# Layer 0's first step: queries, keys and values by whole products, and the x sums of the first sequence formed in step 4

## The chip, the cores and the metric

The kernel runs on one core of a Trainium2 chip. A core has five engines that work side by side, each through its own list of instructions in order: TensorE (PE, matrix products and transposes), VectorE (DVE), ScalarE (ACT), GpSimd (POOL) and SyncE (SP, which here only issues DMA transfers). They wait for one another by semaphores. The metric is the device time of one execution in microseconds (us); less is better. A kernel is timed as the median of several runs.

## The reference

Two transformer layers on x of 4 sequences x 512 rows x 512 columns, all in float32. Each layer normalizes x and adds an attention and a mixture of experts. What matters here is the attention of layer 0:

```
xn = layernorm(x)
q  = rope(rmsnorm(xn @ Wq + bq))        # 16 heads of 128
lk = rope(rmsnorm(xn @ Wlk + blk))      # keys and values of the local window
lv = xn @ Wlv + blv
w  = softmax(xn @ Wcmp + bcmp) over every 4 rows     # compressed entries
entries = sum over 4 rows of w * xn
ck = rope(rmsnorm(entries @ Wk + bk));  cv = entries @ Wv + bv
ctx = top8_attention(q, ck, cv) + window_attention(q, lk, lv)
out = ctx/2 @ Wo + bo
```

The mixture of experts of layer 0 picks two of eight experts for each row by `xn @ Wr`.

## The kernel before

**Tiling.** x lies on chip as 16 tiles of 128 rows (`acc`); sequence b has tiles 4b to 4b + 3. `layernorm(n)` (line 195) makes one tile: row statistics (`bn_stats`, L201, then L203 and L204 on VectorE), the power -1/2 on GpSimd (L205), the scaled rows (L211), a write of these to memory for the experts (L212), four transposes on TensorE (L217) and a copy on ScalarE into `xnT` (L218). `start_sequence(n)` calls it.

**Steps.** Layer 0's attention runs 32 steps: 8 groups of 2 heads, and in each group the 4 sequences; step i is group i // 4 and sequence i % 4. A step projects 512 rows of `xnT` with the group's weights: `w_a` holds the columns of the two heads' queries and of the first head's keys (384 in all), `w_b` the two heads' values and the second head's keys. `project(i)` returns the parts of this. Then come `scores`, `turn`, `context`, `turn_context` and `output` of the step.

**Seven products for eight.** The rows are split in two halves, the columns of x in two halves, and the columns of the weights into `w_a` and `w_b`. The plain product of these 2 x 2 blocks has eight block products. `project` uses a scheme with seven (p1 to p7, `product`, line 552, matmuls at L555), which costs sums: four sums of x (`sums_x`, L545 to L548), sums of the weights per group (`combine_weights`, L106), and sums of products while these leave PSUM (L590, L591, L597, L598, L604, L611 to L619). A block product is 2 blocks of 128 rows x 2 of contraction; one such product shows as two matmul instructions in the profile, so a step has 14 x 4 = 56. `finish` then takes the squares (L459, ScalarE), the norms (L460, L461, GpSimd), the rotation (L468 to L471, VectorE) and the scale (L569, ScalarE); `turn_queries` and `turn_keys` transpose (L575, L581).

**x sums.** They are the same for all groups. In steps 0 to 3 VectorE forms them and SP writes them to memory (`xsd`, L550); from step 4 on `load_sums` reads them back (L530) into four tiles with one buffer each. `combine_weights` overwrites the first half of `w_b` and the bias of `w_b` in place.

**Compressed keys.** `compress(b)` is a generator in four stages, each taken by a `next`: the softmax weights of every four rows (from the logits of `first_logits`, L227 to L234; L479 to L490), their spread to all partitions by a product and the weighted sums of x (`entT`, L493 to L498), keys and values (L503 to L510), the turned keys `ckT` (L513, L514).

**Order.** Ahead of the loop over steps stands a prologue, written out by hand, with the projections of step 0, the four stages of `comp[0]`, the layernorms of tiles 4 to 7 and the logits of sequences 0 and 1. In the loop's iteration i the parts of `project(i + 1)` stand between the parts of the attention of step i, and a list of jobs (`run0`) adds layernorms, routing and experts at places (i, t). In iteration 3 begin the choice of experts (`choose`, `place`). A planner then orders each engine's instructions: of those that its model of time takes as ready, the one earliest in the program goes first, so an instruction that is ready early can float ahead. `keep_in_program_order` pins one behind the instruction written before it on its engine. PSUM tiles with the tag "mm" (all the products here) have three buffers.

Of the kernel before, what the change touches and what calls it, by code (L numbers as in the profile page):

```python
# [12 lines left out]
F32 = mybir.dt.float32  # L13
I32 = mybir.dt.int32
AF = mybir.ActivationFunctionType
ALU = mybir.AluOpType
# [4 lines left out]
P = 128  # L21
B, S, HID = 4, 512, 512
T = B * S
NT = T // P
TC = S // P
KC = HID // P
NH, D = 16, 128
# [17 lines left out]
def two_layers(ctx: ExitStack, tc: tile.TileContext, a: dict, out: bass.AP, large: bass.AP):  # L45
# [3 lines left out]
    V, G, A, PE = nc.vector, nc.gpsimd, nc.scalar, nc.tensor  # L49
# [11 lines left out]
    wk0 = layer0.enter_context(tc.tile_pool(name="att0", bufs=2))  # L61
    setup = ExitStack()

    sp0 = setup.enter_context(tc.tile_pool(name="setup", bufs=2, side="right"))


    def psum(tag, name):
        return ps.tile([P, 512], F32, tag=tag, name=name, bufs={"mm": 3, "sc": 3, "tr": 2}[tag])
# [120 lines left out]
    def unrotated():  # L189


        tc.keep_in_program_order(V.memset(turned, 1.0))
        V.tensor_scalar(turned[R:P, :], wcol[R:P, 0:1], wcol[R:P, 1:2], D * math.sqrt(D), ALU.mult, ALU.mult)

    def layernorm(n, pool, bank):

        pin = tc.keep_in_program_order if n < TC else (lambda x: x)
        st = small.tile([P, 6], F32, tag="st", name=f"st_{n}")  # L200
        pin(V.bn_stats(st, acc[:, n, :]))  # L201
        mv = small.tile([P, 2], F32, tag="mv", name=f"mv_{n}")
        V.bn_aggr(mv, st)  # L203
        V.tensor_scalar(mv[:, 1:2], mv[:, 1:2], 1e-5, None, ALU.add)  # L204
        G.tensor_tensor(mv[:, 1:2], mv[:, 1:2], nhalf[:, 0:1], ALU.pow)  # L205
        made = {}

        def rows():
            tag = "ctx" if n in (2, 3) else "xn"
            xn = made["xn"] = (wk0 if n in (2, 3) else pool).tile([P, HID], F32, tag=tag, name=f"xn_{n}")  # L210
            pin(V.tensor_scalar(xn, acc[:, n, :], mv[:, 0:1], mv[:, 1:2], ALU.subtract, ALU.mult))  # L211
            (nc.scalar if TC <= n < 2 * TC else nc.sync).dma_start(out=xnd[ts(n, P), :], in_=xn)  # L212

        def turn():
            xn, tr = made["xn"], bank("tr", f"trx_{n}")
            for k in range(KC):
                pin(PE.transpose(tr[:, ts(k, P)], xn[:, ts(k, P)], ident))  # L217
            A.copy(xnT[:, :, ts(n, P)], tr.rearrange("p (k t) -> p k t", k=KC))  # L218
        return rows, turn
# [304 lines left out]

    def load_sums(i):

        for n in range(4):
            xs[n] = wk0.tile([P, 2, 256], F32, tag=f"x{n}", name=f"x{n}_{i}", bufs=1)
            if i >= B:
                nc.sync.dma_start(out=xs[n].rearrange("p k t -> p (k t)"), in_=xsd[steps[i][1], n])  # L530

    def project(i):
# [3 lines left out]
        g, b = steps[i]  # L536
# [4 lines left out]
        u, qb, sq = {}, {}, {}  # L541

        def sums_x():
            if i < B:
                V.tensor_tensor(xs[2], x11, x21, ALU.subtract)  # L545
                V.tensor_tensor(xs[0], x21, x22, ALU.add)
                V.tensor_tensor(xs[1], xs[0], x11, ALU.subtract)
                V.tensor_tensor(xs[3], x12, xs[1], ALU.subtract)  # L548
                for n in range(4):
                    nc.sync.dma_start(out=xsd[b, n], in_=xs[n].rearrange("p k t -> p (k t)"))  # L550
# [64 lines left out]
        def fifth():  # L615
            u2 = u["u2"]
            for c in range(2):
                p3 = product("p3", xs3, w_b[:, 2:4, :], c).rearrange("p (h d) -> p h d", d=D)
                V.tensor_tensor(lv[:, c, :, 0:D], p3, by_head(u2)[:, c], ALU.add)  # L619
            x = lv[:, :, 2, 0:D]  # L620
            ss = squares(x, TC, wk0, f"{i}_k", float(D))
            rotate(x, t1[:, :, 2, :], t2[:, :, 2, :], TC, wk0, f"{i}_k")
            for h in range(HG):
                norm_k[(i, h)] = [ss[:, t : t + 1] if h else sq[t // 2][:, ds(t % 2 * 3 + 2, 1)] for t in range(TC)]

        xs0, xs1, xs2, xs3 = (xs[n] for n in range(4))
        return qkT, sums_x, first, second, third, fourth, fifth, turn_queries, turn_keys

# [121 lines left out]
    def first_logits(b):  # L750
        def get(rows_):
            V.tensor_copy(lg0[:, ts(b, TC), :], rows_[:, :, 1:])
        lr, turn = logits(b, wr, sp0, "r0", get, psum)
        turn()
        row_w[b] = lr[0:1, :]
# [4 lines left out]
        return logits(b, rout["rw"], pool, "r1", get, bank)[1]  # L760

    def start_sequence(n):
        for f in layernorm(n, sp0, psum):
            f()

    def add_bo(n):
# [92 lines left out]
        jobs0.append(((len(steps) - 1, b), lambda b=b: second_logits(b, rout["pool"], psum)()))  # L859
    run0 = schedule(jobs0)  # L860

    load_sums(0)
    qkT, sums_x, first, second, third, fourth, fifth, turn_queries, turn_keys = project(0)
    start_sequence(0)
    start_sequence(1)
    def rest():
# [21 lines left out]
        part = load(const, "part", [P, 1], a["c_part"])  # L888
        tables()

    first(rest)
    combine_weights(0)
    unrotated()
    sums_x()
    first_logits(0)
    second(0)
    turn_queries(0)
    second(1)
    third()
    next(comp[0])  # L900
    start_sequence(4)
    start_sequence(5)
    fourth()
    next(comp[0])
    turn_queries(1)
    start_sequence(6)
    fifth()
    next(comp[0])
    turn_keys(0)
    start_sequence(7)  # L910
    next(comp[0])
    first_logits(1)
    for i, (g, b) in enumerate(steps):
        if b == 0:
# [1146 lines left out]
```

## Time and profile before

| | us |
|---|---|
| three runs, median | 2111.65 (2110.91 to 2112.95) |
| profiled execution | 2114.76 |
| its span, first to last instruction | 2112.8 |
| TensorE busy | 2057.1 (97%) |
| VectorE busy | 1463.7 (69%) |
| ScalarE busy | 872.0 (41%) |
| GpSimd busy | 732.8 (35%) |
| mean granted TensorE clock | 0.996 |
| first product of step 0 | starts at 9.77 |
| first scores of step 0 | start at 58.97 |
| first scores of step 3 | start at 200.93 |

The profile is of one execution. All positions in time count from the first instruction. PE is TensorE, PEld its loads of weights, L is a line of the kernel. A line of the timeline gives the start, the duration of the merged stretch, the engine, the line, the operation, output and inputs, the shape, how many instructions, and in brackets how long the engine was idle before it and what ended that. A line of the waits gives who waited for whom, the total, how often, and the longest. A line of the windows gives a stretch, its length, the busy time of PE, PEld, DVE, ACT and POOL with the number of instructions, the granted clock of TensorE, the busy share of the DMA engines, and GB/s. The name `wB` stands there both for the weights of that name and for the spread weights of `compress`.

### The profile page before, as it was taken

What the parts mean: (1) busy time and instruction counts of PE and PEld (TensorE: products, weight loads), DVE (VectorE), ACT (ScalarE), POOL (GpSimd) and SP (SyncE); (2) the same over time, 40 slices, a digit from 0 to 9 for tenths busy, and PEclk for the clock granted to TensorE, in tenths of its full rate; (3) what the DMA queues carried; (4) which work ended last, traced back from release to release, by engine and by line L of the source; (5) the groups of instructions that cost most, each with busy time, mean ns of one, the idle gap of its engine ahead of it and who ended that gap; (6) DMA issues with size and microseconds to landing.
All of it is one profiled execution on the core that took longest, in us unless ns stands there. A gap on an engine that the chain in (4) does not pass through costs nothing.

```text
span 2112.8 us, 27908 instructions
## 1 busy us (share of the span) xinstructions
PE 2057.1 (97%) x9138; PEld 1229.1 (58%) x9138; DVE 1463.7 (69%) x3514; ACT 872.0 (41%) x2661; POOL 732.8 (35%) x722
## 2 busy tenths in 40 slices
PE   7999999999999999999999999999999999999988
PEld 4566666666666666666666666665334445445443
DVE  7978967666766766666676778787486555556775
ACT  3444544444444444444443444444243332333332
POOL 3322244443323333333332344453113432332650
PEclk9999999999999999999999999999999999999999
DMA  7201123323332333343233222221316775673551
GB/s 251 76 31 58 39 97 114 143 100 110 126 127 95 121 136 100 110 141 111 95 134 129 76 70 71 70 90 61 115 57 220 258 239 181 217 239 122 143 167 56
DMA packets 95818, 258.73 MB, mean 122 GB/s; under 512 B 12913, under 2 KB 25201, under 8 KB 85681
## 3 DMA queue, kind: packets, MB, share of 16 engines
q0 software_dynamic: 25712, 139.48, 20.0%
q1 hardware_dynamic: 68800, 115.29, 16.4%
q10 hardware_dynamic: 1152, 2.10, 0.3%
q8 instruction: 75, 1.23, 0.2%
q14 instruction: 79, 0.64, 0.1%
HBM read 212.52 MB, written 44.30 MB: 122 GB/s over the span
## 4 chain that ended last, share of the span: by engine, by line
PE 78%; DVE 9%; issue 4%; ACT 4%; POOL 3%; DMA 2%; SPq 0%; ACTq 0%; POOLq 0%; DVEq 0%
PE p L555 22%; PE hp_r L419 13%; PE op L722 10%; PE st L647 4%; PE qp L1090 3%; PE st L1114 3%; PE sp L638 2%; PE cx L1128 2%; PE trm_r L409 2%; PE o L1197 2%; ACT sq L459 2%; PE ca L691 2%; PE vp L1050 1%; PE trq L575 1%; PE trs L673 1%
## 5 line engine op out<-in xcount | busy, mean ns | idle before, releaser
L722 PE MATMUL op<-Wo,cT 128*128 128x512 f32 x512 | 230.4, 598 | 4.9 <-DVE lv L619 3.1
L419 PE MATMUL hp_r<-we_r,xT_r 128*128 128x512 f32 x520 | 235.0, 595 | 0.0
L655 POOL TENSOR_TENSOR lT<-lT,lmask 128x512 f32<-128x512 f32 (+1 forms) x128 | 156.4, 1234 | 182.5 <-ACT lT L651 182.3
L384 POOL DMA_INDIRECT xr_r<-xnd,rows_r x78 | 101.1, 1296 | 293.0 <-PE trm_r L409 243.9
L555 PE MATMUL p<-wB,x 128*128 128x384 f32 x512 | 176.4, 488 | 4.1 <-DVE u L611 3.4
L555 PE MATMUL p<-wT,x 128*128 128x384 f32 x512 | 179.5, 493 | 0.7 <-DVE wT L106 0.7
L555 PE MATMUL p<-wA,xnT 128*128 128x384 f32 x512 | 173.3, 489 | 0.4 <-DVE u L590 0.4
L722 PEld LDWEIGHTS op<-Wo,cT 128*128 128x128 f32 x512 | 92.0, 190 | 114.6 <-issue 77.2
L459 ACT ACTIVATE sq<-qb 128x128 f32<-128x128 f32 x384 | 119.0, 310 | 89.9 <-DVE qb L604 35.3
L419 PEld LDWEIGHTS hp_r<-we_r,xT_r 128*128 128x128 f32 x520 | 94.8, 190 | 104.5 <-issue 96.0
L1116 ACT ACTIVATE pT<-st 128x1024 f32<-128x1024 f32 x128 | 123.9, 1018 | 68.4 <-PE st L1114 57.4
L725 DVE TENSOR_TENSOR acc<-acc,op 128x512 f32<-128x512 f32 x128 | 87.7, 685 | 72.3 <-PE op L722 72.0
L555 PEld LDWEIGHTS p<-wB,x 128*128 128x128 f32 x512 | 94.0, 190 | 67.5 <-issue 9.6
L555 PEld LDWEIGHTS p<-wT,x 128*128 128x128 f32 x512 | 95.2, 193 | 63.3 <-issue 8.9
L555 PEld LDWEIGHTS p<-wA,xnT 128*128 128x128 f32 x512 | 95.0, 192 | 59.8 <-DVE u L590 1.6
L411 ACT COPY xT_r<-trm_r 128x512 f32<-128x512 f32 x78 | 45.3, 581 | 203.4 <-PE trm_r L409 168.0
L569 ACT ACTIVATE qb<-qb,ss 128x128 f32<-128x128 f32 x256 | 81.9, 390 | 111.6 <-POOL ss L461 108.5
L651 ACT ACTIVATE lT<-st,ss 128x256 f32<-128x256 f32 (+1 forms) x128 | 46.8, 448 | 177.8 <-PE st L647 177.7
L647 PE MATMUL st<-qkT 128*128 128x256 f32 (+1 forms) x512 | 109.3, 354 | 0.0
L434 POOL DMA_INDIRECT row_r<-yd,slot_r x64 | 74.8, 1169 | 96.2 <-DVE row_r L1226 35.5
L647 PEld LDWEIGHTS st<-qkT 128*128 128x128 f32 x512 | 92.0, 191 | 10.9 <-issue 1.0
L461 POOL TENSOR_TENSOR ss<-ss,nhalf 128x6 f32<-128x6 f32 x64 | 95.2, 1488 | 5.3
(320 smaller groups left out, 4334.3 us busy)
## 6 DMA issues: line engine op xcount, KB each, us to landing
x<-xsd SPq DMA_DIRECT2D x112, 256.0 KB
yd<-yr_r SPq DMA_DIRECT2D x78, 256.0 KB
wA<-in_wA SPq DMA_DIRECT2D x16, 384.0 KB
wB<-in_wB SPq DMA_DIRECT2D x16, 384.0 KB
xnd<-xn SPq DMA_DIRECT2D x24, 256.0 KB
accd<-acc SPq DMA_DIRECT2D x18, 256.0 KB
acc<-in_x SPq DMA_DIRECT2D x16, 256.0 KB
Wo<-in_Wo SPq DMA_DIRECT2D x8, 512.0 KB
```

The source lines that it names most:

```text
L384: G.indirect_dma_start(out=out, out_offset=None, in_=src, in_offset=at_rows(idx[:, i : i + 1]))
L419: PE.matmul(hp, lhsT=xT[:, k, :], rhs=w[:, ts(k, HID)], start=(k == 0), stop=(k == KC - 1))
L434: G.indirect_dma_start(out=x, out_offset=None, in_=self.yd, in_offset=at_rows(self.r.slot[:, k, n : n + 1]))
L459: A.activation(sq, x[:, h, :], AF.Square, accum_out=ss[:, h : h + 1])
L461: G.tensor_tensor(ss, ss, nhalf[:, 0:n], ALU.pow)
L555: PE.matmul(p, lhsT=x[:, k, ts(c, P)], rhs=w[:, k, :], start=(k == 0), stop=(k == 1))
L569: A.activation(x[:, j, :], x[:, j, :], AF.Copy, scale=sq[t][:, j : j + 1])
L647: PE.matmul(st[:, ds((t % 2) * 256, n)], lhsT=qkT[:, HG + h, ts(t, P)], rhs=qkT[:, h, ds(t * P, n)], start=True, stop=True)
L655: G.tensor_tensor(dst, dst, lmask.rearrange("p a w j -> p (a w j)")[:, 0:n], ALU.mult)
L722: PE.matmul(op, lhsT=cT[:, h, ts(t, P)], rhs=wo[:, h, :], start=(h == 0), stop=(h == HG - 1))
L725: V.tensor_tensor(acc[:, n, :], acc[:, n, :], op, ALU.add)
L1116: A.activation(pt[:, ts(pair, 2), :], st, AF.Exp, scale=SCALE1)
```

## The change

Step 0 no longer uses the seven products. A new function `whole` makes, for a half of the rows (two blocks of 128), the full product with `w_a` or with `w_b` over all four blocks of the contraction and adds the bias as it leaves PSUM: 16 block products of 128 rows, 64 matmul instructions. `project(0)` returns this in place of the seven products' parts, and the end of `fifth` becomes `local_norms`, which step 0 calls by itself. Step 0 forms no x sums and has no `load_sums`. Steps 1 to 3 are as before; step 4, the next step of sequence 0, forms the sums of sequence 0 and writes them, where it read them before. Step 8 and later read them as before. In the prologue, `combine_weights(0)` stands behind the last whole product, the logits of sequence 0 behind the second pair of query blocks, the first stage of `comp[0]` between the two pairs of value blocks, and the layernorms of tiles 4 to 7 behind the turned keys. For tiles 8 to 15 `start_sequence` pins the row statistics to their place (`hold`).

```diff
-    def layernorm(n, pool, bank):
+    def layernorm(n, pool, bank, hold=False):
...
-        pin(V.bn_stats(st, acc[:, n, :]))
+        (tc.keep_in_program_order if hold else pin)(V.bn_stats(st, acc[:, n, :]))
...
     def load_sums(i):
...
-            if i >= B:
+            if i > B:
                 nc.sync.dma_start(out=xs[n].rearrange("p k t -> p (k t)"), in_=xsd[steps[i][1], n])
...
         def sums_x():
-            if i < B:
+            if i <= B:
                 V.tensor_tensor(xs[2], x11, x21, ALU.subtract)
...
+            local_norms()
+
+        def local_norms():
             x = lv[:, :, 2, 0:D]
...
+        def whole(part_, cs, between=lambda: None):
+
+            made = []
+            for c in cs:
+                p = psum("mm", f"pw{part_}_{c}")[:, 0 : 3 * D]
+                for k in range(KC):
+                    PE.matmul(p, lhsT=xnT[:, k, ds(b * S + c * P, P)], rhs=(w_a, w_b)[part_][:, k, :],
+                              start=(k == 0), stop=(k == KC - 1))
+                made.append((c, p))
+            between()
+            for c, p in made:
+                if part_:
+                    V.tensor_tensor(lv[:, c, :, 0:D], p.rearrange("p (h d) -> p h d", d=D),
+                                    b2[:, 1, :].rearrange("p (h d) -> p h d", d=D), ALU.add)
+                    continue
+                if c % 2 == 0:
+                    qb[c // 2] = wk0.tile(rows3, F32, tag="qb", name=f"qb{c // 2}_{i}")
+                V.tensor_tensor(qb[c // 2][:, c % 2, :], p, b2[:, 0, :], ALU.add)
+                if c % 2:
+                    finish(c // 2)
+
+        if i == 0:
+            return qkT, whole, local_norms, turn_queries, turn_keys
...
     def start_sequence(n):
-        for f in layernorm(n, sp0, psum):
+
+        for f in layernorm(n, sp0, psum, hold=n >= 2 * TC):
             f()
...
-    load_sums(0)
-    qkT, sums_x, first, second, third, fourth, fifth, turn_queries, turn_keys = project(0)
+    qkT, whole, local_norms, turn_queries, turn_keys = project(0)
...
-    first(rest)
+    whole(0, (0, 1), rest)
+    unrotated()
+    whole(0, (2, 3))
+    first_logits(0)
+    whole(1, (0, 1))
+    next(comp[0])
+    turn_queries(0)
+    whole(1, (2, 3))
     combine_weights(0)
-    unrotated()
-    sums_x()
-    first_logits(0)
-    second(0)
-    turn_queries(0)
-    second(1)
-    third()
-    next(comp[0])
-    start_sequence(4)
-    start_sequence(5)
-    fourth()
+    local_norms()
     next(comp[0])
     turn_queries(1)
+    turn_keys(0)
+    start_sequence(4)
+    next(comp[0])
+    start_sequence(5)
+    next(comp[0])
     start_sequence(6)
-    fifth()
-    next(comp[0])
-    turn_keys(0)
     start_sequence(7)
-    next(comp[0])
     first_logits(1)
```

## The prediction

> **What bounds the kernel now.** I read the page's engine table first. TensorE (PE) is busy for 97% of the span and VectorE (DVE) for 69%, so over the whole program TensorE sets the time, and a change can win only where TensorE waits, runs at a lower clock, or does less.
>
> ```profile
> PE 2057.1 (97%) x9138; PEld 1229.1 (58%) x9138; DVE 1463.7 (69%) x3514; ACT 872.0 (41%) x2661; POOL 732.8 (35%) x722
> ...
> PE   7999999999999999999999999999999999999988
> ```
>
> The span is 2112.8, so TensorE idles 55.7 us in all; much of that lies in the first of the 40 slices, in which the first step's projections are made. So the second view is the waits of TensorE over the first 200 us:
>
> ```profile
> PE trx L217 <- DVE xn L211: 8.0, 3, 5.9
> PE trq L575 <- ACT qb L569: 3.1, 3, 2.0
> PE wB L493 <- DVE wd L490: 1.5, 1, 1.5
> ```
>
> The 5.9 and 1.9 in the first line are the load and the layernorm of the first rows, ahead of any product, and are not touched. The third view is TensorE's timeline (start, duration, what, idle before it and its releaser), from the second product group on:
>
> ```profile
> 18.04 3.60 PE L227 MATMUL lg_r<-xnT,wr 128*9 128x512 f32 x8 [0.76 <-ACT xnT L218]
> 22.34 0.41 PE L234 MATMUL trg_r<-ident,lr_r 9*128 9x9 f32 x4 [0.69 <-ACT lr_r L229]
> 24.79 0.33 PE L575 MATMUL trq<-ident,qb 128*128 128x128 f32 x1 [2.04 <-ACT qb L569]
> ...
> 26.86 8.39 PE L555 MATMUL p<-wT,x 128*128 128x384 f32 x16 [0.70 <-DVE wT L106]
> 35.09 2.74 PE L555 MATMUL p<-wT,xnT 128*128 128x384 f32 x8
> ...
> 43.64 0.33 PE L575 MATMUL trq<-ident,qb 128*128 128x128 f32 x1 [0.85 <-ACT qb L569]
> 44.23 0.63 PE L575 MATMUL trq<-ident,qb 128*128 128x128 f32 x3 [0.25 <-ACT qb L569]
> ```
>
> Read the 16 matmuls at 26.86 against the 8 at 35.09: the first take 0.51 us each, the others 0.32. TensorE had only the small transposes to do from 21.6 on, then waited for the weight sums, and started those products at half clock. The fourth view, windows of 2 us (last but two: granted clock), says so, and shows VectorE full at its start (third pair):
>
> ```profile
> 24.00:26.00 2.00, 1.21 (x8) 1.00 (x8) 1.72 (x5) 1.28 (x4) 0.30 (x1) 1.00 1.06 406
> 26.00:28.00 2.00, 1.30 (x4) 0.84 (x3) 2.00 (x4) 0.97 (x3) 0.00 (x0) 0.51 1.05 389
> 28.00:30.00 2.00, 2.00 (x4) 1.01 (x3) 0.98 (x4) 0.00 (x0) 0.00 (x0) 0.50 1.05 386
> 30.00:32.00 2.00, 2.00 (x4) 1.01 (x3) 0.84 (x4) 0.00 (x0) 0.00 (x0) 0.50 0.75 249
> 32.00:34.00 2.00, 2.00 (x6) 1.15 (x5) 1.35 (x4) 0.00 (x0) 0.55 (x1) 0.78 0.15 40
> ```
>
> So the stretch from 18 to 45 is set by sums on VectorE (of x, then of the weights) that stand ahead of the products.
>
> **The change part by part.** The unit: 12 matmuls from 184.07 to 187.94 at full clock give 0.3225 us each.
>
> *Products.* Seven products of 8 matmul instructions (56) become 64 in whole products: 8 x 0.3225 = +2.58 us, on TensorE, which is the path.
>
> *Slow clock.* The 16 matmuls from 26.86 to 35.09 took 8.23 where 16 x 0.3225 = 5.16 would do: 3.07 lost; the windows give the same, 1.30 x 0.49 + 4 x 0.50 + 2 x 0.22 = 3.08. Whole products need only transposed rows and weights as loaded, so from 18 on TensorE has 16 + 8 + 32 instructions without a sum ahead of them, some 19 us of work. I take -3.07; ends: 0 if TensorE starves again, -3.07.
> The Trainium skill, "TensorE: Matmul & The Clock Gate", Part 1, says that the clock is halved after an idle window of about 3.4 us and given back after about 3.4 us of sustained work. That speaks for less than I take: a stretch of 3.4 us at half clock costs 1.7, and the sum would end 1.37 us higher. The clock row here shows half clock for nearly 7 us, and the row decides.
>
> *Waits of 18 to 45.* 0.69 + 2.04 + 0.70 + 0.85 + 0.25 = 4.53 of idle go, because each stands before work that whole products can precede. The 0.76 before the logits stays: it is the transposed copy of rows 256 on, now needed by the second pair of blocks. Ends: 0 and -4.53 - 0.76; I take -4.53.
>
> *VectorE in the first step.* Out: the four x sums (0.83 + 1.21 + 0.88 + 0.68 = 3.60) and, of 9.58 us of evictions and u sums (12 of 0.53 to 0.56, two double ones of 0.95, two of 0.55), all but 8 of 0.55 = 4.40. Relief 8.8 us. It is worth nothing by itself; it lets the layernorms of rows 512 to 1023 fill the gaps, and later waits get shorter. Between 60 and 72 TensorE waits 0.70 (for a copy), 0.49 and 1.50 (for VectorE); I take half of these 2.69, -1.3; ends 0 and -2.69.
>
> *What is late next.* The weight sums overwrite the weights of keys and values in place, so they now wait for the last whole product and stand, pinned, ahead of the compressed keys' products. I follow that chain: TensorE from 18.0: 16 (5.2), logits (3.5), transposes (0.9), 32 (10.3) ends near 37.9; the broadcast of the softmax weights ends at 39.3. VectorE: weight sums left 0.96 + 0.95 + 0.94 + 0.55 = 3.4, key rotation 1.4, eight steps of the entries at 0.6 start to start 4.8, so 48.9; values product 1.1; from there to the compressed keys 4.3 as before (53.3 to 57.63). That is 54.3. TensorE's own work up to the first scores: from 9.77 to 58.97 it has 49.20 less 5.32 idle less 3.07 slow = 40.81; plus 2.58, plus the 0.76 that stays, ends at 53.92. So a new wait of about 0.4, and I take +0.8 since some of the fill is not ready in time. Ends: 0, and +6.2 if the layernorms of rows 512 to 1023 (four of 0.68 + 0.17 + 0.14 + 0.55) all fall into that chain too.
>
> *Step 4 (counted from 0).* It reads no stored sums; VectorE makes them in the iteration of step 3, where the choice of experts begins: 4 x 0.68 = 2.7, bounded by 3.6, the first step's own sums beside a busy GpSimd. That iteration begins near 200. In 194 to 203 VectorE is busy 6.22 of 9.00, and the tiles are free by then (their last reader is at 190.93 to 192.2), so that idle covers them; with the cover gone, in the stretch 203 to 212 (8.93 of 9.00), all of it would show. I take +0.5; ends 0 and +3.6.
> The Trainium skill, "SBUF — State Buffer", Who interferes with whom, says that a VectorE instruction with two SBUF inputs and a GpSimd instruction that reads SBUF block one another wholly. By that four mask products of GpSimd (mean 1.23) could stand before four sums: 4.9 in place of 0.5, and the whole sum would be -0.6. The sums of 18 to 23 beside GpSimd's tables cost 0.9 more in all, so I keep to the rows.
>
> *Queues.* SP: four writes of sums leave 38.30 (2.12 us of issue); behind them stood the second group's weights, used from 245 on, so nothing is gained. They return near 200; behind them stand reads of stored sums for step 5, issued at 220.05, first used past 253. The four reads of 176.62 to 192.41 go; the weights behind them come earlier, unneeded. ACT: four row writes (0.34 each) move by some us; their reader is past 269. GpSimd: the four powers (0.55) of the moved layernorms are inside the layernorm above. The memset and scale of `turned` (0.3) and the logits move with nobody behind them before the keys. All 0.
>
> *Pinned statistics.* Eight bn_stats of rows 1024 on are held at their place. The one at 40.56 stood early, in VectorE's fullest stretch: -0.66 if that place was on the path, +0.7 if its later place delays the transposes behind it, as at 67.48. I take 0.
>
> Sum: 2.58 - 3.07 - 4.53 - 1.3 + 0.8 + 0.5 = **-5.0 us**. The profiled execution took 2114.76 (span 2112.8, 1.96 around it) and would take 2109.7; it stands 3.1 above the median 2111.65, from which the same sum gives **2106.6**.
>
> **The rivals.** 0.2% (4.2 us) is about what this measurement can tell from no change; so faster is below 2107.4, slower above 2115.9.
>
> A, the compressed keys take the place of the old waits. For it: VectorE was busy 9.96 of 10 from 40 to 50 and the chain above ends 0.4 after TensorE's own work. Against it: 8.8 us less VectorE work before it. With half of its 6.2 in the way and no relief later: 2.58 - 3.07 - 4.53 + 3.1 + 0.5 = -1.4, 2110.2.
>
> B, the relief goes further: no wait of 18 to 72 is left and step 4's sums are covered. 2.58 - 3.07 - 4.53 - 0.76 - 2.69 = -8.5, 2103.2. Against it: the 0.76 is a copy on ACT that nothing here moves.
>
> C, slower: the statistics of rows 512 to 1023, not pinned, float into the idle VectorE time and stand there until their rows land. Place: 17 to 23. By the windows 5.5 MB had moved by 20 us, and about 6.1 MB were issued up to those rows' last load, so I estimate its landing near 22; a stop of 5 us holds the evictions, three PSUM banks fill, TensorE starves and its clock halves again. Then the 3.07 and 4.53 stay, and +2.58 and up to +3.6 remain: +2.6 to +6.2, 2116.0 at +4.4. It decides as soon as the stop is longer than the some 5 us that two free banks (2.58 each) cover. Against it: the planner then had to place them that early; before, the first stood at 26.79.
>
> **How the numbers follow.** Chances: my forecast 0.50 (own range 2104.5 to 2108.8, three quarters of it below 2107.4), A 0.23, B 0.17, C 0.10 (half of it above 2115.9). Faster 0.37 + 0.17 + 0.02 of A = 0.56; slower 0.05; same the rest, 0.39. The likeliest is 2106.6. The range runs from B's end with 1 us of spread, 2102, to 2112, short of A's worst (all 6.2 in the way: +1.7, 2113.3), which leaves out C and a little of A.
>
> **What would show it.** Right: 16 wA matmuls in one piece from 9.77; granted clock 1.00 in all windows from 16 to 50; no wait of 2 us before the first query transposes; first scores near 54 instead of 58.97; 64 product instructions in the first step; x sums of step 4 between 192 and 205 with no wait of TensorE over 1 us behind them. Wrong: a clock of 0.5 anywhere after 16, a wait before the scores for `ckT`, VectorE stopped on a load of `acc` near 20, or a different order of the later steps that brings waits where none were.

## The result, and the profile after

The changed kernel takes 2125.55 us (median of four runs, 2125.31 to 2125.68); the kernel before, on the same chip, takes 2111.95 (2110.91 to 2112.95). The ratio is 1.0064, 95% interval 1.0047 to 1.0082: 13.6 us slower. The forecast was 5.0 us faster. The profiled execution took 2125.46, span 2123.6.

The page of the changed kernel, its engine table and TensorE's row of the 40 slices:

```profile
span 2123.6 us, 27903 instructions
PE 2062.8 (97%) x9146; PEld 1233.7 (58%) x9146; DVE 1461.1 (69%) x3506; ACT 870.7 (41%) x2661; POOL 731.5 (34%) x722
...
PE   7899999999999999999999999999999999999998
```

The span grew by 10.8 over that of before: TensorE is busy 5.7 longer and idle 5.1 longer (60.8 against 55.7). The page doesn't say where. The first scores of each step (first matmul of L665) do, since they mark the same point of the work in both traces:

| first scores of step | 0 | 1 | 2 | 3 | 4 | 5 |
|---|---|---|---|---|---|---|
| before, us | 58.97 | 105.91 | 155.43 | 200.93 | 242.53 | 284.25 |
| after, us | 68.39 | 117.41 | 168.15 | 212.67 | 254.27 | 296.00 |
| difference | +9.42 | +11.50 | +12.72 | +11.74 | +11.74 | +11.75 |

All of the loss is there by 170 us: 9.42 in the prologue, 2.08 and 1.22 in the iterations of steps 0 and 1, of which that of step 2 gives 0.98 back. From step 4's first scores to the end of the span it is 1870.2 before and 1869.3 after, so this point is the cleaner measure; the rest scatters by some us from run to run (1866.8 to 1872.1 over all the kernels below).

TensorE's timeline of the changed kernel from the second pair of blocks to the first scores, columns as in the timeline shown of before:

```profile
22.65 3.60 PE L227 MATMUL lg_r<-xnT,wr 128*9 128x512 f32 x8
26.18 2.20 PE L636 MATMUL pw<-wB,xnT 128*128 128x384 f32 x6
31.23 0.41 PE L234 MATMUL trg_r<-ident,lr_r 9*128 9x9 f32 x4 [2.85 <-ACT lr_r L229]
31.57 5.18 PE L636 MATMUL pw<-wB,xnT 128*128 128x384 f32 x10
...
37.74 5.33 PE L636 MATMUL pw<-wB,xnT 128*128 128x384 f32 x16
42.91 1.02 PE L493 MATMUL wB<-wd,ones_sq 128*128 128x512 f32 x2
...
51.90 0.91 PE L556 MATMUL p<-wA,xnT 128*128 128x384 f32 x2 [1.03 <-DVE u L591]
...
54.62 0.49 PE L503 MATMUL kv<-wk,entT 128*128 128x128 f32 x2 [0.93 <-DVE entT L498]
56.74 0.49 PE L503 MATMUL kv<-wk,entT 128*128 128x128 f32 x2 [1.63 <-DVE entT L498]
...
61.15 0.47 PE L513 MATMUL trck<-ident,ck 128*128 128x128 f32 x1 [3.03 <-ACT ck L510]
61.42 1.91 PE L217 MATMUL trx<-ident,xn 128*128 128x128 f32 x8
64.00 4.46 PE L227 MATMUL lg_r<-xnT,wr 128*9 128x512 f32 x8 [0.68 <-ACT xnT L218]
68.39 1.16 PE L665 MATMUL sp<-ckT,qkT 128*128 128x32 f32 x8
```

The whole products themselves are dense, as forecast: 16 of them take 5.33 at 37.74. Two waits frame them. At 31.23 the turned logits wait 2.85 for a copy on ScalarE; the ten products behind it take 5.18 where ten at full clock take 3.23. At 61.15 the compressed keys wait 3.03, after three shorter waits for VectorE. And the work that could have filled that wait, the transposes at 61.42 and the logits of sequence 1 at 64.00, stands behind the waiting instruction in TensorE's list. It runs only then, and the scores come 7.2 after the turned keys.

The windows of 2 us (last but two: granted clock) show half clock at three places, two ahead of the first scores and one in the iteration of step 0:

```profile
30.00:32.00 2.00, 0.77 (x5) 0.75 (x6) 0.19 (x1) 1.18 (x4) 0.43 (x1) 0.91 0.63 175
32.00:34.00 2.00, 2.00 (x4) 1.04 (x4) 0.56 (x1) 0.13 (x1) 0.00 (x0) 0.50 0.87 285
34.00:36.00 2.00, 2.00 (x6) 1.04 (x5) 0.00 (x0) 0.28 (x2) 0.00 (x0) 0.74 0.96 283
...
58.00:60.00 2.00, 0.12 (x2) 0.00 (x0) 1.14 (x6) 1.56 (x6) 0.60 (x2) 0.74 0.00 0
60.00:62.00 2.00, 0.85 (x4) 0.85 (x5) 0.00 (x0) 0.75 (x3) 0.58 (x2) 0.50 0.00 0
62.00:64.00 2.00, 1.33 (x7) 0.92 (x5) 0.02 (x1) 1.20 (x3) 0.00 (x0) 0.50 0.00 0
64.00:66.00 2.00, 2.00 (x3) 0.39 (x4) 1.97 (x3) 0.00 (x0) 0.00 (x0) 0.56 0.23 86
...
78.00:80.00 2.00, 0.90 (x2) 0.53 (x3) 2.00 (x9) 0.00 (x0) 0.62 (x1) 0.86 0.00 0
80.00:82.00 2.00, 2.00 (x4) 0.88 (x4) 1.79 (x6) 0.00 (x0) 0.56 (x1) 0.50 0.00 0
82.00:84.00 2.00, 2.00 (x12) 1.44 (x11) 2.00 (x5) 0.35 (x1) 0.00 (x0) 0.79 0.38 131
```

By busy time x (1 - clock) the first stretch costs 2.00 x 0.50 + 2.00 x 0.26 + 0.77 x 0.09 = 1.6, the second 0.85 x 0.50 + 1.33 x 0.50 + 2.00 x 0.44 = 2.0, the third, 0.90 x 0.14 + 2.00 x 0.50 + 2.00 x 0.21, 1.5. Half clock has come back, at three new places. The first stands behind the wait of 2.85. The second begins near 58.9, only 0.8 us into the wait of 3.03, so the row of shorter waits ahead of it has its part in it. The third follows a wait of 2.58 for the spread of the next softmax weights (`wd`, L490), at 79.10.

VectorE's timeline of the changed kernel shows why the keys are late:

```profile
31.68 0.19 DVE L779 COPY lg_r<-trg_r 128x32 f32<-128x32 f32 x1 [2.28 <-PE trg_r L234]
33.22 0.56 DVE L642 TENSOR_TENSOR lv<-pw,b 128x384 f32<-128x384 f32 x1 [1.35 <-PE pw L636]
36.79 0.56 DVE L642 TENSOR_TENSOR lv<-pw,b 128x384 f32<-128x384 f32 x1 [3.01 <-PE pw L636]
...
43.10 0.56 DVE L642 TENSOR_TENSOR lv<-pw,b 128x384 f32<-128x384 f32 x1 [2.02 <-PE pw L636]
43.58 0.95 DVE L106 TENSOR_TENSOR wT<-wB 128x768 f32<-128x768 f32 x1
...
48.60 0.68 DVE L497 TENSOR_TENSOR prod<-xnT,wB 128x512 f32<-128x512 f32 x1
...
56.00 0.68 DVE L498 TENSOR_REDUCE entT<-prod 128x128 f32<-128x512 f32 x1
```

From 29.4 to 43.1, while TensorE makes whole products, VectorE has almost nothing to do: 10.0 us idle in six pieces, four of them in these lines. Then everything stands in one row: weight sums and key rotation from 43.58 to 48.60, the entries from 48.60 to 56.68. It is full from 43.1 to 58.

### The profile page after: what moved, and what is told of

Read it like the earlier page. It is cut to its first block, busy times and chain, and to the rows that moved or that the text cites. A ratio compares the mean times of both kernels' runs of the same rounds, so it can differ in the third digit from the quotient of the medians.

```text
span 2123.6 us, 27903 instructions
## 1 busy us (share of the span) xinstructions
PE 2062.8 (97%) x9146; PEld 1233.7 (58%) x9146; DVE 1461.1 (69%) x3506; ACT 870.7 (41%) x2661; POOL 731.5 (34%) x722
## 4 chain that ended last, share of the span: by engine, by line
PE 76%; DVE 10%; issue 4%; ACT 4%; POOL 3%; DMA 2%; SPq 0%; ACTq 0%; POOLq 0%; DVEq 0%
PE p L556 21%; PE hp_r L419 12%; PE op L749 10%; PE st L674 4%; PE qp L1115 3%; PE st L1139 3%; PE sp L665 3%; PE cx L1153 2%; PE ca L718 2%; PE o L1222 2%; PE trm_r L409 2%; ACT sq L459 1%; PE vp L1075 1%; PE trs L700 1%; PE lg_r L227 1%
## 5 line engine op out<-in xcount | busy, mean ns | idle before, releaser
L682 POOL TENSOR_TENSOR lT<-lT,lmask 128x512 f32<-128x512 f32 (+1 forms) x128 | 156.5, 1235 | 198.1 <-ACT lT L678 197.9
L556 PE MATMUL p<-wB,x 128*128 128x384 f32 x496 | 170.6, 488 | 3.6 <-DVE u L612 2.9
L556 PE MATMUL p<-wT,x 128*128 128x384 f32 x496 | 172.0, 489 | 0.0
L556 PE MATMUL p<-wA,xnT 128*128 128x384 f32 x496 | 166.2, 487 | 1.5 <-DVE u L591 1.4
L556 PEld LDWEIGHTS p<-wA,xnT 128*128 128x128 f32 x496 | 91.6, 190 | 59.5 <-DVE u L591 2.8
L674 PEld LDWEIGHTS st<-qkT 128*128 128x128 f32 x512 | 92.2, 191 | 10.8 <-issue 1.0
```

Of the source, the lines that this page charges most:

```text
L556: PE.matmul(p, lhsT=x[:, k, ts(c, P)], rhs=w[:, k, :], start=(k == 0), stop=(k == 1))
L674: PE.matmul(st[:, ds((t % 2) * 256, n)], lhsT=qkT[:, HG + h, ts(t, P)], rhs=qkT[:, h, ds(t * P, n)], start=True, stop=True)
L682: G.tensor_tensor(dst, dst, lmask.rearrange("p a w j -> p (a w j)")[:, 0:n], ALU.mult)
```

## The experiments

I had three causes to tell apart, all of them places in the order, none the products:

- **Copy**: the logits' copy (L229) stands on ScalarE behind the squares and scales of the second query pair, and TensorE waits for it at 28.4.
- **Chain**: entries and compressed keys run too late, behind the weight sums, and TensorE's fill is written behind the wait for the keys.
- **Pins**: the row statistics of tiles 8 to 15, held at their places in the iterations, can't use VectorE's idle time in the prologue.

Against these stands the rival that the loss is something else, the sums of step 4 above all. Times below are medians, each with the ratio to the kernel before in the same job; "step 4" is the difference of step 4's first scores from the 242.53 of before. The two columns on the right are from one trace each. In these traces step 0's first product starts between 8.98 and 10.33, which no edit touches, so differences of under some 1.4 us in these columns say little. The lengths of the iterations are free of that.

| kernel | time | before | ratio (95%) | first scores, step 0 | step 4 |
|---|---|---|---|---|---|
| changed | 2125.55 | 2111.95 | 1.0064 (1.0047 to 1.0082) | 68.39 | +11.74 |
| no hold | 2121.73 | 2113.09 | 1.0036 (1.0024 to 1.0049) | 67.36 | +6.96 |
| logits first | 2122.46 | 2113.09 | 1.0045 (1.0028 to 1.0062) | 65.18 | +9.36 |
| weights late | 2117.54 | 2113.09 | 1.0024 (1.0014 to 1.0033) | 56.62 | +2.58 |
| step 4 alone | 2112.41 | 2113.09 | 0.9997 (0.9987 to 1.0006) | 58.51 | -0.64 |
| weights late, no hold | 2110.12 | 2113.25 | 0.9983 (0.9974 to 0.9993) | 56.55 | -4.95 |
| the same, logits first | 2107.97 | 2113.25 | 0.9975 (0.9965 to 0.9985) | 55.70 | -6.05 |
| keys early | 2108.06 | 2113.25 | 0.9980 (0.9970 to 0.9990) | 53.27 | -7.10 |
| old places | 2104.60 | 2113.25 | 0.9958 (0.9942 to 0.9975) | 51.97 | -8.42 |
| pins alone, on before | 2114.30 | 2113.86 | 1.0001 (0.9992 to 1.0011) | 59.01 | -0.02 |
| old places with pins | 2109.71 | 2113.86 | 0.9982 (0.9973 to 0.9992) | 49.87 | -5.52 |
| old places, sums early | 2105.92 | 2113.86 | 0.9971 (0.9961 to 0.9981) | 54.37 | -6.86 |

### One cause at a time

One difference between the traces is not the edits'. Up to the wait at the logits, the changed kernel, no hold and weights late have the same instructions in the same order on TensorE, VectorE, ScalarE and GpSimd. Still their traces differ there. The changed kernel:

```profile
9.23 6.29 PE L636 MATMUL pw<-wA,xnT 128*128 128x384 f32 x16
```

No hold:

```profile
9.37 7.78 PE L636 MATMUL pw<-wA,xnT 128*128 128x384 f32 x16
...
30.86 0.41 PE L234 MATMUL trg_r<-ident,lr_r 9*128 9x9 f32 x4 [1.51 <-ACT lr_r L229]
```

The first 16 products are slower here (in weights late they take 7.32), TensorE comes to the logits 1.0 us later, and the wait is 1.51 (in weights late 1.42) in place of 2.85, without half clock behind it. So the whole products end 2.1 us earlier in both traces, and these 2.1 us belong to the execution, not to the edit. The four timed runs of the changed kernel lie within 0.4 us, but only one of them has a trace; how often it starts so isn't known.

**No hold.** The changed kernel without its pins:

```diff
-        for f in layernorm(n, sp0, psum, hold=n >= 2 * TC):
+        for f in layernorm(n, sp0, psum, hold=False):
```

> The changed kernel with the row statistics of tiles 8 to 15 no longer pinned. Theory 'chain' (the start is late because the compressed keys' sums on VectorE stand behind the weight sums, and the fill of TensorE behind them): nothing of that is touched, so the time stays within 1.5 us of the changed kernel's 2125.5 and the first scores within 0.5 us of 68.39. Theory 'pins' (the held statistics stand in the way): 3 us or more come back, 2122 or less. Theory 'copy' (the copy of the logits, late on ScalarE): no change either.

Measured: the loss against the kernel before falls from 13.6 to 8.6 us; step 4's first scores come 4.78 earlier. Most of it is not in the prologue (first scores -1.03) but behind it: the iteration of step 0 takes 45.68 in place of 49.02, that of step 1 49.51 in place of 50.74. VectorE's timeline of this run, in the stretch that was idle:

```profile
28.94 0.68 DVE L201 BATCH_NORM_STATS2 st<-acc 128x6 f32<-128x512 f32 x1
...
31.50 0.66 DVE L201 BATCH_NORM_STATS2 st<-acc 128x6 f32<-128x512 f32 x1
...
32.69 1.28 DVE L201 BATCH_NORM_STATS2 st<-acc 128x6 f32<-128x512 f32 x2
```

Four statistics of tiles 8 on go into the idle time near 30, which in the changed kernel stood pinned in the iterations (78.82, 89.75, 96.77, 101.48). In the changed kernel that idle time is left unused. With them gone, the wait for `wd` in the iteration of step 0 is 1.61 in place of 2.58, and no half clock follows it.

**Logits first.** The logits of sequence 0 ahead of the second query pair, nothing else:

```diff
-    whole(0, (2, 3))
     first_logits(0)
+    whole(0, (2, 3))
```

> The changed kernel with the logits of sequence 0 written ahead of the second pair of query blocks, so that their copy on ScalarE no longer stands behind the second pair's squares and scales. Theory 'copy': the wait of 2.85 us ahead of the turned logits falls below 1.7 and the half clock of 31 to 36 goes; the whole products end 3 to 4.5 us earlier than 42.9 and the first scores come 3 to 4.5 us earlier than 68.39; time 2121 to 2122.5. Theory 'chain' alone: the products end earlier but the scores hardly do (under 1 us), because VectorE sets them; time 2124.5 or more.

Measured: the loss falls from 13.6 to 9.4, and the first scores come 3.21 earlier, step 4's 2.38. TensorE's timeline of this run:

```profile
24.51 0.41 PE L234 MATMUL trg_r<-ident,lr_r 9*128 9x9 f32 x4
...
39.65 1.02 PE L493 MATMUL wB<-wd,ones_sq 128*128 128x512 f32 x2
...
57.89 0.48 PE L513 MATMUL trck<-ident,ck 128*128 128x128 f32 x1 [3.02 <-ACT ck L510]
...
65.18 1.05 PE L665 MATMUL sp<-ckT,qkT 128*128 128x32 f32 x7
```

The wait of 2.85 and its half clock are gone, and everything up to the scores moves forward by 3.2, the wait for the keys unchanged at its end. The whole products end 3.26 earlier (39.65 for 42.91), and that goes straight through. So Copy is a cause of its own. Its size is open: against no hold and weights late, whose products end at 40.84 and 40.78 with the copy at its old place, 39.65 is only 1.1 to 1.2 earlier.

**Weights late.** The weight sums and the last two stages of the compressed keys behind the layernorms of tiles 4 to 7, with pins:

```diff
     whole(1, (2, 3))
-    combine_weights(0)
     local_norms()
     next(comp[0])
...
     start_sequence(4)
-    next(comp[0])
     start_sequence(5)
-    next(comp[0])
     start_sequence(6)
     start_sequence(7)
+    next(comp[0])
+    combine_weights(0)
+    next(comp[0])
     first_logits(1)
```

> The changed kernel with the weight sums of group 0 written behind the compressed keys' third stage, and tiles 6 and 7 ahead of it. Theory 'chain': the sums for the compressed keys start near 45 instead of 48.6 and the keys are ready near 57 instead of 62; the wait of 3.03 us ahead of the turned keys and the half clock of 59 to 66 go; first scores 61 to 63 instead of 68.39; time 2118 to 2121. Theory 'copy': the wait of 2.85 us stays and with it most of the loss; first scores not before 67, time 2124 or more. Theory 'pins': no change, 2125.

Measured: first scores at 56.62, 11.77 earlier, step 4's 9.16 earlier; the loss falls from 13.6 to 4.5. Of the 11.77, 2.1 are there when the whole products end, ahead of anything that the edit moves; some 9.6 are the edit's, more than expected. Part comes back in the iteration of step 0, which takes 50.57 in place of 49.02. The two longest waits of TensorE between 56 and 108, in this run:

```profile
PE wB L493 <- DVE wd L490: 2.3, 1, 2.3
PE trx L217 <- DVE xn L211: 1.9, 1, 1.9
```

The weight sums now run from 54.42 to 59.5 on VectorE, behind which the softmax weights and the pinned statistics of this iteration (first at 70.27) come late. After these waits the clock is 0.50 from 72 to 74 and 0.67 from 74 to 76, 1.7 more.

**Weights late, no hold.** The order of weights late, and

```diff
-        for f in layernorm(n, sp0, psum, hold=n >= 2 * TC):
+        for f in layernorm(n, sp0, psum, hold=False):
```

> Two edits to the changed kernel together: weight sums of group 0 behind the compressed keys (as in e3_weights_late), and the row statistics of tiles 8 to 15 not pinned (as in e1_no_hold). If the two losses are separate and add up: first scores near 56.6 and the iteration of step 0 back from 50.6 us to 46 to 48, so the scores of step 3 start at 198 to 200 against 200.93 before, and the time is within 2 us of the kernel before. If the pins only mattered because the start was late: the iteration of step 0 stays near 50 us and the time 4 us above the kernel before.

Measured: the iteration of step 0 falls to 44.36. The only wait of TensorE that the same stretch shows, in this run:

```profile
PE trq L576 <- ACT sT L702: 1.9, 1, 1.9
```

Both waits of the run before are gone, for one of 1.9. At step 4's first scores the two edits give 16.69, alone 4.78 and 9.16: together 2.75 more than their sum. The iterations show it more cleanly: without the pins that of step 0 is 3.34 shorter in the changed kernel and 6.21 shorter in the order of weights late, where the chain's work has been moved to behind the first scores. Chain and Pins are both causes, and they aggravate one another. The kernel is 3.1 us faster than before, more than the 2 that was expected at most.

**Step 4 alone.** The kernel before, only the sums of the first sequence formed in step 4 (step 0 forms its own but doesn't write them):

```diff
-            if i >= B:
+            if i > B:
...
-            if i < B:
+            if i <= B:
...
-                for n in range(4):
+                for n in range(4 if i else 0):
```

> The kernel before with one part of the change alone: step 4 forms and writes the x sums of sequence 0 (the first step still forms them for its seven products, but does not write them). If VectorE's idle time covers them, as the traces of both kernels say (the iteration of step 3 is 41.60 us long in both): 2112 within 1 us. If the four sums of 0.68 us stand on the path: 2114 to 2116.

Measured: ratio 0.9997. The iteration of step 3, which forms the sums, takes 41.60, as before, to the hundredth. The window where the prediction had looked for cover, in this run:

```profile
194.00:203.00 9.00, 8.98 (x36) 5.44 (x35) 8.06 (x31) 3.90 (x15) 2.37 (x4) 1.00 0.59 195
```

VectorE is busy 8.06 where it was 6.22, and TensorE is as busy as before, 8.98. The rival that the loss comes from step 4 is out.

**Pins alone.** The kernel before, with the pins:

```diff
-        for f in layernorm(n, sp0, psum):
+        for f in layernorm(n, sp0, psum, hold=n >= 2 * TC):
```

> The kernel before with one part of the change alone: the row statistics of tiles 8 to 15 pinned to their place. Theory 'pins cost by themselves' (statistics that had filled idle VectorE time early now stand in the full iterations of steps 0 and 1): these two iterations grow from 46.94 and 49.52 us by 2 to 4 us together, time 2 to 5 us above the kernel before. Theory 'pins cost only where the prologue leaves VectorE idle' (in the kernel before only the one at 40.56 stood early): within 1.5 us of the kernel before.

Measured: ratio 1.0001, step 4's first scores -0.02. In the old order, whose trace shows only one of the eight early (40.56), holding them costs nothing: the iteration of step 1 is 1.22 longer, those of steps 0 and 2 are 0.74 and 0.79 shorter. The price of the pins is what the whole products would have freed.

### Towards an order that keeps the gain

**Weights late, no hold, logits first.** The kernel weights late without hold, and

```diff
-    whole(0, (2, 3))
     first_logits(0)
+    whole(0, (2, 3))
```

> As e5_late_no_hold, with the logits of sequence 0 also written ahead of the second pair of query blocks (as in e2_logits_first): the wait of 1.4 us ahead of the turned logits goes as well. If it is separate too, first scores and time come 1 to 3 us earlier than in e5_late_no_hold, and the kernel is 0 to 4 us faster than before. If VectorE sets the first scores, they do not move.

Measured: 2107.97. The logits' place gives 1.10 more at step 4 (-6.05 against -4.95), less than half of its 2.38 in the changed kernel. In the order of weights late the wait at the logits' transposes is 1.11, without a half clock behind it, and with the logits first it is still 1.30, now at 24.5, since only four products of the second query pair stand between the logits and their transposes. So there was little to win. The whole products end 0.86 earlier (39.66 for 40.52) and the first scores come 0.85 earlier, about the 1.1 to 1.2 of logits first against no hold and weights late; all of this is within the scatter of the start.

**Keys early.** Entries as early as their inputs allow, the sums right behind the turned keys, layernorms of tiles 4 to 7 and the logits of sequence 1 last, no hold:

```diff
+    first_logits(0)
+    next(comp[0])
     whole(0, (2, 3))
-    first_logits(0)
+    next(comp[0])
+    turn_queries(0)
     whole(1, (0, 1))
     next(comp[0])
-    turn_queries(0)
     whole(1, (2, 3))
-    combine_weights(0)
+    next(comp[0])
     local_norms()
-    next(comp[0])
     turn_queries(1)
     turn_keys(0)
+    combine_weights(0)
     start_sequence(4)
-    next(comp[0])
     start_sequence(5)
-    next(comp[0])
     start_sequence(6)
...
```

> Whole products with all four stages of the compressed keys written between them (logits first, spread weights and entries ahead of the value products), weight sums behind, no pins. Theory 'chain': the keys no longer end last; they are ready near 45 and the first scores start when TensorE's own work ends, at 53 to 56; time 3 to 6 us below the kernel before, as predicted for the change. If the value products and their evictions, now later, set the local keys and values instead: iteration of step 0 longer by 2 us or more, time within 2 us of the kernel before.

Measured: 2108.06, first scores at 53.27. The weight sums stand ahead of the layernorms again, as in the changed kernel, and the logits of sequence 1 are again written last. With the entries early, the keys are turned at 43.20 in place of 61.15, after a wait of 1.1 in place of 3.0; ahead of it TensorE waits 0.3 and 0.2, and behind it not at all until the scores. So fill written behind the keys costs nothing once the keys don't make TensorE wait.

**Old places.** Whole products, and every other part near the place that it had in the old prologue, no hold:

```diff
     whole(0, (0, 1), rest)
     unrotated()
+    first_logits(0)
     whole(0, (2, 3))
-    first_logits(0)
+    turn_queries(0)
+    next(comp[0])
+    start_sequence(4)
+    start_sequence(5)
     whole(1, (0, 1))
     next(comp[0])
-    turn_queries(0)
+    turn_queries(1)
+    start_sequence(6)
     whole(1, (2, 3))
-    combine_weights(0)
     local_norms()
     next(comp[0])
-    turn_queries(1)
     turn_keys(0)
-    start_sequence(4)
+    start_sequence(7)
     next(comp[0])
-    start_sequence(5)
-    next(comp[0])
-    start_sequence(6)
-    start_sequence(7)
+    combine_weights(0)
     first_logits(1)
```

> Whole products alone: layernorms of tiles 4 to 7 and the compressed keys stay at the places that they had between the seven products, only the weight sums stand at the end, no pins. If the price of the change lies in the order written around the products and not in the eight more matmul instructions: no wait over 2 us, first scores 53 to 56, time 3 to 6 us below the kernel before. If whole products themselves cost: time equal to the kernel before or above.

Measured: 2104.60, 8.65 us faster than the kernel before: this beats both kernels, and by more than the 3 to 6 us expected. TensorE's timeline of this run:

```profile
30.76 4.68 PE L636 MATMUL pw<-wB,xnT 128*128 128x384 f32 x14
35.28 1.02 PE L493 MATMUL wB<-wd,ones_sq 128*128 128x512 f32 x2
...
37.01 5.33 PE L636 MATMUL pw<-wB,xnT 128*128 128x384 f32 x16
42.17 0.61 PE L503 MATMUL kv<-wk,entT 128*128 128x128 f32 x4
...
46.44 3.60 PE L227 MATMUL lg_r<-xnT,wr 128*9 128x512 f32 x8
49.97 0.33 PE L513 MATMUL trck<-ident,ck 128*128 128x128 f32 x1
...
51.97 1.05 PE L665 MATMUL sp<-ckT,qkT 128*128 128x32 f32 x8
```

The entries run beside the last whole products (the spread of the weights at 35.28, the first keys product at 42.17), and the logits of sequence 1 stand ahead of the turned keys and fill the time until `ck` is there. TensorE's waits from the first instruction to the first scores, in this run:

```profile
PE trx L217 <- DVE xn L211: 8.3, 2, 5.9
PE pw L636 <- ACT xnT L218: 0.2, 1, 0.2
```

Only the first rows' load and layernorm are left, and one of 0.2.

**Old places with pins**, and **old places, sums early** (`combine_weights(0)` right behind the last whole product, as in the change):

```diff
-        for f in layernorm(n, sp0, psum, hold=False):
+        for f in layernorm(n, sp0, psum, hold=n >= 2 * TC):
```

> The kernel e8_old_places with the pins put back. If pins cost where the prologue leaves VectorE idle: the iterations of steps 0 and 1 grow from 45.67 and 49.52 us by 3 to 6 us together and the time is 2107 to 2111 against some 2104.6. If their price hung on the late start: within 1.5 us of e8_old_places.

```diff
     whole(1, (2, 3))
+    combine_weights(0)
     local_norms()
...
-    combine_weights(0)
     first_logits(1)
```

> The kernel e8_old_places with the weight sums of group 0 at the place that the change gives them, right behind the last whole product, and the compressed keys' entries still ahead of the second pair of value blocks. Theory 'chain': the entries no longer stand behind the weight sums, so that place costs little: first scores within 1.5 us of 51.97, time within 2 us of e8_old_places. If the place of the weight sums costs by itself: first scores 3 us later or more, as much of the 11.8 us that e3_weights_late gained there.

Measured: with the pins the gain falls from 8.65 to 4.15; the iteration of step 0 goes from 45.67 to 49.46 and that of step 1 from 49.52 to 51.56, while the first scores come 2.10 earlier, of which 1.35 is an earlier first product (8.98 for 10.33). With the early sums the gain is 7.94, the first scores 2.40 and step 4's 1.56 later. That is more than the 1.5 expected at the first scores if the place costs little, and less than the 3 if it costs by itself. The two gains differ by less than their intervals, so the place of the sums alone is at most a small part in an order where the entries begin before them.

## Why the prediction was wrong

*Products.* Right as far as can be read: 64 instructions, 16 at full clock in 5.33 (0.33 each). Old places shows the idea at work: with them, TensorE has no wait and no half clock between 18 and the first scores, and the gain is 8.4 at step 4, somewhat more than the 5.0 taken.

*Slow clock, -3.07.* The loss at 26 to 32 went, and 1.6 + 2.0 = 3.6 came back ahead of the first scores, at 32 to 36 and 58 to 66, and 1.5 more behind them. The step that failed is the argument that TensorE has 56 instructions from 18 on without a sum ahead of them. It counted sums only. The four transposes of the logits, which stand between them, wait for a copy on ScalarE. That this wait drew half clock was in part chance of the execution: with the same list the traces of no hold and weights late show it at 1.51 and 1.42, without half clock.

*Waits of 18 to 45, -4.53.* Of the five waits that were to go, those for the queries and the weight sums went, but 0.69 at the logits became 2.85. I had put it among the waits that "whole products can precede". They don't precede it by enough: TensorE's list holds six products of the value pair ahead of the transposes, 2.2 us of work, and ScalarE's list holds the copy behind the second query pair's work, 4.4 us after the logits. ScalarE's timeline of the changed kernel:

```profile
29.44 1.28 ACT L570 ACTIVATE qb<-qb,ss 128x128 f32<-128x128 f32 x4 [1.74 <-POOL ss L461]
30.62 0.56 ACT L229 COPY lr_r<-lg_r 9x512 f32<-9x512 f32 x1
```

The logits are complete at 26.25; the copy comes at 30.62, behind four scales which wait 1.74 for the norms from GpSimd. The diff moved the logits behind the second query pair, and I had costed that move on TensorE and not on ScalarE.

*What is late next, +0.8.* This is the step that failed worst. The chain was the right one, every link late. The whole products end near 43.0 in place of 37.9: 2.85 of wait and 1.6 of half clock are 4.4 of these 5.1. The entries take 8.1 in place of 4.8, since two layernorm scalings and step 1's evictions (L591, L592, L468) lie between their eight steps on VectorE. So the last entry is at 56.7 and the turned keys at 61.2, where I had 54.3. Then comes what I had left out of the sum altogether: I took TensorE's own work up to 53.92 as fill that can stand ahead of the wait. In the list 8 transposes and 8 logits products stand behind it, 7.0 us (61.42 to 68.39) with their own wait and half clock.

*Relief of VectorE, -1.3.* Wrong in sign. The relief was there, 10.0 us idle between 29 and 43, but nothing was allowed into it: the chain's work was written later, and the statistics were pinned. The iteration of step 0 grew by 2.08 where shorter waits were expected. TensorE's waits there add up to 3.4, where they were 3.2 (the one for `wd` went from 1.50 to 2.58, others went away); most of the 2.08 is the 1.5 of half clock behind that wait. In old places it is 1.27 shorter than before, about the size I had taken.

*Pinned statistics, 0.* Wrong. In the iterations of steps 0 to 2 together, where the start of the trace doesn't count, the pins cost 3.77 in the changed kernel, 7.46 in the order of weights late, 5.02 in old places, and nothing (-0.31) on the kernel before. I had weighed the one that stood early in the old order, not those that the new idle time would have drawn in.

*Step 4, +0.5.* Measured nothing (-0.64 at step 4 where it stands alone, and iterations of 41.60 in both). Where they stand in the changed kernel: 191.46, 203.42, 209.81 and 211.03, somewhat past the forecast 192 to 205, since that iteration began 11.7 later; TensorE waits 0.6 once between 190 and 215. *Queues, 0*: step 4 alone, which moves the writes and reads of the sums, runs in the time of before.

The sum for the prologue, by the changed kernel's own rows from TensorE's first product to the first scores: idle and half clock were 5.32 + 3.07 = 8.39 and are 11.37 + 3.6 = 15.0, so +6.6; products +2.58; the first product starts 0.54 earlier. That is +8.6 of the measured +9.42. Some 0.8 I can't assign.

The rivals: A named the mechanism (the compressed keys take the place of the old waits), but I gave its worst case +1.7, because its price held VectorE's layernorms alone and neither the logits' copy nor the fill behind the wait nor the pins. B needed another order; old places goes as far, 8.65. C, statistics that stand until their rows land, was the slower one that I had, and did not happen: the statistics of rows 512 on stand at 21.2 to 27.9 in the changed kernel, none of them after a wait for a load.

Of the signs that I had named for a wrong forecast, two came: a clock of 0.5 after 16, and a wait ahead of the scores for the compressed keys.

What stays open: the parts of Chain weren't run one by one in the changed kernel. Weights late moves the sums, the last two stages and the layernorms past one another; the sums' place alone was moved only in the order of old places, where its 1.56 at step 4 is hardly more than the scatter. And the size of Copy lies between 1.1 and 3.3 us, by whether its wait draws half clock.

## What to carry to other kernels

When a change relieves an engine, ask for each instruction that could use the freed time whether the order lets it: pinned work and work that is written later can't, and then the relief is only a gap ahead of a jam. Follow a moved product on every engine that touches its result, not on TensorE alone; here one copy of 0.56, behind the wrong neighbours, cost between 1.1 and 3.3 us up to the end of the whole products. And when a chain's end is compared with "the other work until then", look up on which side of the waiting instruction that work stands in the list.

## What the hardware showed that I had not expected

The granted clock. In the changed kernel the wait of 2.85 that ends at 31.23 is followed by half clock. Waits of 1.51, 1.42 and 1.11 at the same instruction (no hold, weights late, weights late without hold) are not: their windows from 32 to 36 show 1.00. But the length of one wait doesn't decide: before the change half clock followed a wait of 2.04. What the four cases share is how little TensorE did in the 3.41 us ahead: it was busy for 0.57 before the drop at 31.64, 1.38 before that at 58.94, 0.83 before that at 79.43, and 1.37 before that at 26.05 in the kernel before. Over all 13 traces no half clock begins with more than 1.61 us of work in the 3.41 ahead of it. A window of 2 us that shows 0.91 has been at half clock for 0.18 of its length, one that shows 0.74 for 0.52; so the half clock after 31.64 lasts 2.00 x (0.18 + 1 + 0.52) = 3.4 us. The one of before, by the same reading, lasts 6.8, twice as long. The Trainium skill, "TensorE: Matmul & The Clock Gate", Part 1, gives an idle window of about 3.4 us for the halving and about 3.4 us of work for the return. The 3.4 agrees with the length here. That the window must be idle does not agree, and the measurement decides: here TensorE was busy for up to 1.38 of it.

Four small instructions on VectorE (`wd`, L490, 128 x 128 each) took 0.93 together at 39.31 in the changed kernel, with GpSimd idle in the window from 38 to 40, and 2.68 at 76.27, with GpSimd busy 1.69 of the 2.00 from 76 to 78. TensorE waits 2.58 for the latter at 79.10. No run was made for the reason, but the traces point at GpSimd's mask products (L682, in the kernel before L655). Over the traces of all 13 kernels, 38 of the 208 `wd` instructions take 1.08 to 1.36 us; each of them overlaps a mask product and ends 0.13 to 0.15 us after it. The other 170 take 0.36 at most.
